# A fused attention and convolution kernel: the last attention slot computes its sums by transfers and most of its products in parts

## The chip, the cores and the metric

The kernel runs on one core of a Trainium2 chip. The metric is the device time of one execution in microseconds (us); less is better. The core has a matrix engine (PE, with its weight loads listed apart as PEld), a vector engine (DVE), an activation engine (ACT), a general engine (POOL) and a queue that issues transfers (SP). Each works through its own list in order; they meet at semaphores. Transfers run on 16 DMA engines and are issued by SP, ACT or POOL. PE writes into eight banks of PSUM, each 128 partitions by 512 columns in float32; everything else lives in SBUF or in main memory (HBM).

## The reference

The input x is (4, 64, 64, 256) in float32: four images of 4096 pixels (tokens) with 256 channels. Layer 0 is full attention inside an image, layer 1 a depthwise convolution with an MLP and a local attention. Cut to what matters:

```python
# layer 0, per image: N = 4096 tokens, q and k have 32 channels
q, k, v = x @ Wq + bq, x @ Wk + bk, x @ Wv + bv
attn = softmax(q @ k.T)                       # 4096 x 4096
x = gamma * (attn @ v) + x

# layer 1
perceived = depthwise_conv3x3(x, w_perc)      # 3 outputs for each of 256 channels
hid = gelu(perceived @ w_up1.T + b_up1)       # 768 -> 512
x_new = x + hid @ w_up2.T + b_up2             # 512 -> 256
qkv = x_new @ w_qkv.T + b_qkv
out = x_new + local_attention_3x3(qkv)
```

## The kernel before, in words

**Slots.** The tokens are cut into 32 blocks of 512 queries (eight image rows of one image). Slot s computes layer 0 for block s, and beside it layer 1 of earlier blocks: the convolution of block s - 2 on DVE, the MLP of block s - 3, the local attention of block s - 5. Lists of jobs, written out by hand, say which piece of layer 1 runs at which of the 16 points of a slot. There is no planner: the order of the Python program is the order on every engine. After slot 31 a tail runs the layer 1 that is left.

**A point of a slot.** The keys of the image come in eight blocks of 512, each worked in two half groups of 256 keys (two key tiles of 128). Half group n (0 to 15) is worked over several points. Two points ahead, PE computes the energies (line 418) and ACT the exponentials p (line 423). One point ahead, p is prepared: added to the sums, and split where that is wanted. At point n, PE multiplies p with the values (`product`, line 481), and the result of 16 half groups gathers in PSUM. At each point the order on PE is: energies of a later half group, the jobs of layer 1, the product. On DVE it is: what the jobs need, then `add_up` for the next half group, then some steps of the convolution (line 687).

**Products in one piece or in parts.** A product of float32 operands is recorded as two matmuls per 512 columns. In parts, p is split into a rounded high part (ACT, lines 428 and 437), a low part (DVE, lines 510 and 446) and a scaled gap (DVE, lines 520 and 447), and three matmuls of the float32r type replace the two; they need values that are split in the same way and read back from HBM. The high and low products go to two accumulators, the gaps to two more, so that a slot with parts holds four PSUM banks; `evacuate` (lines 564 and 567) joins them with two ACT and two DVE operations. `IN_PARTS` names the seven even half groups whose two tiles are both in parts (n = 2, 4, ..., 14); `ONE_IN_PARTS` names the odd ones of which the second tile is in parts, `BOTH_IN_PARTS` those of which the first tile is, too. `in_two_sums(s)`, `full(s)`, `in_parts` and `alone` decide which slots and half groups follow these lists. Before the change slot 31 follows none of them: all its products are in one piece.

**Sums of the weights.** The softmax needs the sum of p over all keys. In the middle slots the half groups that `by_dma` names are added by transfers that accumulate into two buffers (`send`, lines 498 and 500, issued by POOL); DVE adds only the last ones and the two buffers (lines 513, 516, 528, 529). Before the change slot 31 has none of these: DVE adds each of its 16 half groups (line 516 once, line 513 fourteen times).

**The values.** `project_v` computes the values of a block ahead of time, for the next image during the last slot of an image (for image 3 that is slot 23), and writes them to HBM: whole (`packed_v`, by ACT, lines 363 and 364), and in forms for the parts (`packed_h`, `packed_f`, `packed_o`, by POOL). For blocks 24 to 31 it writes the whole values of every pair of tiles, since slot 31 reads them all.

**Buffers.** Tiles have tags, and each tag a fixed ring of buffers: three for p, one each for ph, pl, pg, four for vs, two for xc, four for the convolution's outputs (perc). A tile that is asked for waits until the last reader of the buffer's previous tile is done. `late_tile` hands out thirds of one perc buffer, `spare` hands out other buffers that have gone out of use. PSUM: two banks for the energies, two banks m for jobs, four banks acc for the products. In the tail the energies' banks become two job banks more, and `turns` gives out the three kinds in rotation.

**Slot 31 and the tail.** Slot 31 has a longer list of jobs: it also runs the MLP of block 29 (`hidden_part`, line 800, at points 8 to 11; hid_a, hid_bc, hid_de and hid_gf are its products), so the convolution of block 29 has to be complete at point 8; then the convolution of block 30 (`upper`) runs, without its last row, which needs the result of slot 31. At the end the sums are closed (`partial_sums`, lines 547 and 550), one fold matmul (dps, line 576) and a reciprocal (line 579) give the factor, and `finish` (lines 590 and 596) scales the result. The tail then does the last row of block 30 and the convolution of block 31 on DVE, while PE runs what is ready of blocks 29 to 31.

Of the kernel before, what the change touches and what calls it, by code (L numbers as in the profile page):

```python
# [16 lines left out]
P = 128  # L17
# [5 lines left out]
NB = 512  # L23
RB = NB // W
WARM = 10
NBLK = N // NB
# [10 lines left out]
NHC = HID // P  # L37
# [5 lines left out]
NSLOT = B * NBLK  # L43
# [9 lines left out]
ONE_IN_PARTS = (1, 3, 5, 7, 9, 11, 13, 15)  # L53
# [5 lines left out]
LAG_PERC, LAG_HID, LAG_ATT = 2, 3, 5  # L59
# [3 lines left out]
def attention_then_perception_kernel(  # L63
# [37 lines left out]
    def unshifted():  # L101
# [6 lines left out]
        def tile_of(shape, tag, name, bufs=1):  # L108
            return pool.tile(shape, F32, tag=tag, name=name, bufs=bufs)

        def bank(tag, name):
            return psum.tile([P, NB], F32, tag=tag, name=name, bufs=dict(m=2, acc=2 * CH)[tag])
# [3 lines left out]
        turns = ["m"]  # L116
# [50 lines left out]
        for r in range(KR):  # L167
            m = near[r * KW : (r + 1) * KW]
# [48 lines left out]
        packed_o = tc.dram_tile([P, NSLOT, 2, 2, C], F32, name="packed_o")  # L217

        def in_two_sums(s):
            return 0 < s < NSLOT - 1 and s != LAG_PERC  # L220

        def full(s):
            return in_two_sums(s) and s > 1 and s % NBLK < NBLK - 1

        def in_parts(s, G, half):
            return in_two_sums(s) and 2 * G + half in IN_PARTS

        def alone(s, n):

            return [i for i, ns in enumerate((BOTH_IN_PARTS, ONE_IN_PARTS)) if full(s) and n in ns]  # L230

        def load_parts(to, s, which):
# [68 lines left out]
        def block(s, G):  # L301
            return s - s % NBLK + G
# [5 lines left out]
        def load_values(s, G):  # L308
            values[s, G] = tile_of([P, TPB, C], "v", f"v_{s}_{G}", 2)
            to = values[s, G].rearrange("p t c -> p (t c)")  # L310
            at = block(s, G)
            if not in_two_sums(s):
                nc.sync.dma_start(out=to, in_=packed_v[:, bass.ts(at, TPB * C)])
            elif full(s):
                nc.sync.dma_start(out=to, in_=packed_h[:, at])
            else:
                nc.sync.dma_start(out=to[:, : 2 * C], in_=packed_h[:, at, : 2 * C])
                nc.sync.dma_start(out=to[:, 2 * C :], in_=packed_v[:, bass.ts(2 * at + 1, 2 * C)])
# [23 lines left out]
        def project_v(s, pair, tag="m"):  # L342
            xc = staged[s]
            ps = bank(tag, f"v_{s}_{pair}")
            for i in range(2):
                for kin in range(CH):
                    nc.tensor.matmul(  # L347
                        ps[:, i * C : (i + 1) * C],
                        lhsT=xc[:, kin, bass.ts(2 * pair + i, P)], rhs=wv[:, kin, :],
                        start=(kin == 0), stop=(kin == CH - 1),  # L350
                    )
            of = ps.rearrange("p (t c) -> p t c", c=C)
            n = 2 * (s % NBLK) + pair
            split, one, both = (n in ns for ns in (IN_PARTS, ONE_IN_PARTS, BOTH_IN_PARTS))
            h = packed_h[:, s, bass.ts(pair, 2 * C)].rearrange("p (t c) -> p t c", c=C)
            if not split or s < NBLK or s >= NSLOT - NBLK:
                if s >= NBLK:
                    v = fresh(f"vs_{s}_{pair}")
                else:
                    if (0, s) not in values:  # L360
                        values[0, s] = tile_of([P, TPB, C], ("v", "vf")[s % 2], f"v_0_{s}", 2)
                    v = values[0, s][:, 2 * pair : 2 * pair + 2, :]
                nc.scalar.activation(v, of, AF.Identity, scale=SPLIT / (SPLIT + 1.0))  # L363
                nc.scalar.dma_start(
                    out=packed_v[:, bass.ts(2 * s + pair, 2 * C)],
                    in_=v.rearrange("p t c -> p (t c)"),
                )
                if not split and not both:
                    tiles = slice(0, 1 if one else 2)
                    nc.gpsimd.dma_start(out=h[:, tiles], in_=v[:, tiles])  # L370
            if not split and not one:
                return
            high = fresh(f"vh_{s}_{pair}")
            if split:
                lg = tile_of([P, 2, NB], "sent", f"vlg_{s}_{pair}")
                lg = lg.rearrange("p f (t c) -> p f t c", c=C)
                low, gap = lg[:, 0], lg[:, 1]
                to = h, packed_f[:, s].rearrange("p f (t c) -> p f t c", c=C)
            elif both:
                low, gap = (fresh(f"v{x}_{s}_{pair}") for x in "lg")  # L380
                lg = low
                to = h, packed_o[:, s, :, 0]
            else:
                high, of = high[:, 0:1], of[:, 1:2]
                lg = fresh(f"vlg_{s}_{pair}")
                low, gap = lg[:, 0:1], lg[:, 1:2]
                to = h[:, 1:2], packed_o[:, s, 1]
            nc.scalar.copy(low, of)
            nc.scalar.activation(high.bitcast(F32R), of, AF.Identity, scale=BELOW)
            nc.vector.tensor_tensor(low, low, high, ALU.subtract)  # L390
            nc.vector.scalar_tensor_tensor(gap, low, -SPLIT, high, ALU.mult, ALU.add)
            nc.vector.tensor_scalar(low, low, SPLIT, None, ALU.mult)
            for at, part in zip(to, (high, lg)):
                nc.gpsimd.dma_start(out=at, in_=part)
            if both:
                nc.gpsimd.dma_start(out=packed_o[:, s, :, 1], in_=gap)
# [88 lines left out]
                started[s].add(to)  # L485

        def by_dma(s, n):
            if full(s):
                return n in BY_DMA_IF_FULL and (n > 1 or s % NBLK > 0)
            return 0 < s < NSLOT - 1 and (s < 2 or s % NBLK < NBLK - 1) and n in BY_DMA  # L490

# [133 lines left out]
        percs, mixes, hids, hs = {}, {}, {}, {}  # L625
# [11 lines left out]
        def late_tile(name):  # L637

            if not thirds:
                t = perc_tile(name).rearrange("p s n -> p (s n)")  # L640
                thirds[:] = [t[:, i * NB : (i + 1) * NB] for i in range(3)]
            return thirds.pop(0)
# [4 lines left out]
                return tile_of([P, TPB, C], tag, name, 2).rearrange("p (a t) c -> p a (t c)", a=2)  # L647
            return tile_of([P, 2, NB], tag, name)

        spares = {NSLOT - 2: ["ph", "pl", "pg"], NSLOT - 1: ["v", "v", "vf"]}  # L650

        def perceive(s, steps):

            at = ring(s) - 1
            percs.setdefault(s, {})

            def begin(i):
                if s >= NSLOT - LAG_PERC:

                    if i % 2 == 0:  # L660
                        percs[s, i] = spare(s, f"perc_{s}_{i}")
                    percs[s][i] = percs[s, i - i % 2][:, i % 2, :]
                else:
                    upper, j = divmod(i, MULT)
                    if not upper:
                        mixes[s, j] = perc_tile(f"perc_{s}_{j}")
                    percs[s][i] = mixes[s, j][:, 2 * upper : 2 * upper + 2, :].rearrange(
                        "p s n -> p (s n)"
                    )
                tap_of(i, 0, 0, RB)  # L670

            def tap_of(i, tap, r0, r1):
                half, j = divmod(i, MULT)
                dy, dx = divmod(tap, 3)
                if s < NSLOT - LAG_PERC:
                    acc = percs[s][i][:, :RUN]
                    win = xp[:, half, bass.ds((at + dy) * WP + dx, RUN)]
                else:
                    acc = percs[s][i].rearrange("p (h w) -> p h w", w=W)[:, r0:r1, :]
                    win = xv[:, half, at + dy + r0 : at + dy + r1, dx : dx + W]  # L680
                wt = wperc[:, half, j, tap : tap + 1]
                if tap == 0:
                    nc.scalar.activation(  # L683
                        acc, win, AF.Identity, bias=bperc[:, half, j : j + 1], scale=wt
                    )
                else:
                    nc.vector.scalar_tensor_tensor(acc, win, wt, acc, ALU.mult, ALU.add)  # L687

            for i, tap, *rows in steps:
                if tap is None:  # L690
                    t = mixes[s, i][:, :, : ROWS - 2]
                    to, a, b, op = rows
                    nc.vector.tensor_tensor(t[:, to, :], t[:, a, :], t[:, b, :], op)  # L693
                    yield
                elif tap > 0:
                    tap_of(i, tap, *rows)
                    yield
                elif i not in percs[s]:
                    begin(i)
# [515 lines left out]
        for slot in range(NSLOT):  # L1215
# [52 lines left out]
            for point in range(points):  # L1268
                G, half = divmod(point, 2)
# [96 lines left out]
        def spread_bank(name):  # L1366
            return spread.tile([P, NB], F32, tag="s", name=name, bufs=2)

        turns[:] = [lambda name: bank("acc", name), spread_bank, "m"]
        last = NSLOT - 1  # L1370
        conv = perceive(last, whole)

# [454 lines left out]
```

## Time and profile before

| | |
|---|---|
| median of 3 runs | 3207.92 us (3205.68 to 3211.80) |
| profiled execution | 3206.14 us |
| its span, first to last instruction | 3204.3 us |
| busy over the span | PE 99%, DVE 91%, ACT 49%, POOL 24% |
| slot 30 (2862.0 to 2957.3) | PE busy 95.1 of 95.3 us, DVE 92.1, ACT 49.8 |
| slot 31 (2957.3 to 3091.0) | PE busy 133.7 of 133.7 us, DVE 112.8, ACT 46.5 |
| tail (3091.0 to 3204.3) | PE busy 103.4 of 113.3 us, DVE 69.1, ACT 30.5 |

How to read it: a line of the timeline gives the start, the length, the engine, the source line, the operation, output and inputs by the program's names, the number of instructions merged, and in brackets how long the engine was idle before and what ended that. The ends of matmuls are modelled and overlap with what follows, so the time that a group of matmuls takes is the distance from its start to the start of the next group. Times count from the start of the span. A mean over the span hides that slot 30, slot 31 and the tail are limited in different ways; the windows show them apart.

### The profile page before, as it was taken

The page shows a single profiled execution, that of the slowest core. Times are in us where ns is not written, and L with a number is a line of the kernel's source. Part 1 is how long each engine was busy: PE and PEld are TensorE (multiplying, and loading weights), DVE is VectorE, ACT ScalarE, POOL GpSimd, SP SyncE. Part 2 cuts the span into 40 slices and gives each one's busy share as a digit, 9 for nine tenths or more (in the row PEclk, how much of TensorE's full clock was granted, in tenths as well). Part 3 has the DMA queues.
Part 4 walks back from the last instruction along what each step waited for, and adds up shares of the span by engine and source line. Part 5 has one row for each costly group of instructions (what it writes and reads, how often), then busy time and mean ns, then how long its engine had stood idle before and what let it go on. Part 6 is the DMA issues. An engine that isn't in the chain of part 4 may idle for free.

```text
span 3204.3 us, 39564 instructions
## 1 busy us (share of the span) xinstructions
PE 3178.9 (99%) x12600; PEld 2269.4 (71%) x12600; DVE 2919.9 (91%) x4306; ACT 1580.8 (49%) x2173; POOL 753.5 (24%) x1052
## 2 busy tenths in 40 slices
PE   9999999999999999999999999999999999999998
PEld 5557777767777777776777777777677777777655
DVE  4878999998999999998999999999899999999894
ACT  4435555445555555544555555554555545555332
POOL 3301122222222221222122232211221223222121
PEclk9999999999999999999999999999999999999999
DMA  8768888877888888877888888886888888888100
GB/s 253 233 171 223 228 230 227 227 230 235 223 232 246 245 223 227 229 207 249 237 221 230 230 243 236 236 233 196 275 234 226 224 230 229 239 240 223 50 25 28
DMA packets 319446, 690.89 MB, mean 216 GB/s; under 512 B 100784, under 2 KB 101824, under 8 KB 319104
## 3 DMA queue, kind: packets, MB, share of 16 engines
q1 hardware_dynamic: 246608, 442.24, 43.0%
q0 software_dynamic: 64944, 232.59, 32.7%
q10 hardware_dynamic: 7680, 13.44, 1.2%
q8 instruction: 105, 1.72, 0.2%
q14 instruction: 109, 0.89, 0.1%
HBM read 419.01 MB, written 81.66 MB: 156 GB/s over the span
## 4 chain that ended last, share of the span: by engine, by line
PE 88%; DVE 8%; DMA 1%; issue 1%; ACT 1%; SPq 1%; ACTq 0%; DVEq 0%; POOL 0%; POOLq 0%
PE acc L481 43%; PE e L418 7%; PE dx L857 6%; PE hid_bc L800 5%; PE hid_gf L800 5%; PE hid_de L800 5%; PE lv L1022 3%; DVE perc L687 3%; PE g L953 3%; PE v L347 3%; PE lo L1155 3%; PE hid_a L800 2%; PE s L1062 2%; PE qk L272 1%; PE hid L832 1%
## 5 line engine op out<-in xcount | busy, mean ns | idle before, releaser
L687 DVE SCALAR_TENSOR_TENSOR perc<-xp,wb,perc 128x526 f32<-128x526 f32 (+1 forms) x1356 | 938.1, 759 | 0.4 <-ACT perc L683 0.2
L423 ACT ACTIVATE p<-e 128x1024 f32<-128x1024 f32 x512 | 524.3, 1024 | 487.6 <-PE e L418 387.9
L481 PE MATMUL acc<-p,v 128*128 128x512 f32 x1372 | 630.1, 594 | 0.2 <-ACT v L363 0.2
L500 POOL DMA_DIRECT2D sent<-p x304 | 257.9, 855 | 1347.3 <-ACT p L423 939.6
L481 PEld LDWEIGHTS acc<-p,v 128*128 128x128 f32 x1372 | 255.4, 190 | 242.6 <-issue 231.9
L418 PE MATMUL e<-qa,ka 128*128 128x512 f32 x1024 | 357.2, 430 | 4.5 <-DMA ka<-st 1.5
L428 ACT ACTIVATE ph<-p 128x1024 fp32r<-128x1024 f32 x203 | 215.1, 1059 | 197.8 <-PE acc L481 118.8
L510 DVE TENSOR_TENSOR pl<-p,ph 128x1024 fp32r<-128x1024 f32 x203 | 252.8, 1246 | 16.7 <-ACT ph L428 16.7
L481 PE MATMUL acc<-ph,v 128*128 128x512 f32 x812 | 264.5, 447 | 0.1
L520 DVE SCALAR_TENSOR_TENSOR pg<-pl,ph 128x1024 fp32r<-128x1024 f32 x203 | 253.8, 1250 | 11.6 <-PE e L418 0.5
L418 PEld LDWEIGHTS e<-qa,ka 128*128 128x128 f32 x1024 | 190.3, 188 | 86.6 <-issue 42.9
L857 PE MATMUL dx<-hid,wup 128*128 128x512 f32 x512 | 230.0, 592 | 0.0
L481 PE MATMUL acc<-pl,vf 128*128 128x512 f32 x812 | 223.2, 397 | 0.0
L481 PE MATMUL acc<-pg,vf 128*128 128x512 f32 x812 | 218.3, 391 | 3.0 <-DVE pg L520 3.0
L437 ACT ACTIVATE oh<-p 128x512 fp32r<-128x512 f32 x200 | 126.0, 630 | 140.6 <-DVE perc L687 61.3
L693 DVE TENSOR_TENSOR perc<-perc 128x262 f32<-128x262 f32 x360 | 179.6, 513 | 6.3
L481 PEld LDWEIGHTS acc<-ph,v 128*128 128x128 f32 x812 | 148.2, 189 | 51.5 <-issue 26.8
L481 PEld LDWEIGHTS acc<-pg,vf 128*128 128x128 f32 x812 | 152.3, 188 | 39.5 <-DVE pg L520 4.7
L481 PEld LDWEIGHTS acc<-pl,vf 128*128 128x128 f32 x812 | 152.9, 188 | 37.5
L823 ACT ACTIVATE hid<-hid,bup 128x512 f32<-128x512 f32 x120 | 80.2, 715 | 199.4 <-DVE hid L807 199.4
L481 PE MATMUL acc<-oh,v 128*128 128x512 f32 x400 | 174.6, 517 | 0.0
L857 PEld LDWEIGHTS dx<-hid,wup 128*128 128x128 f32 x512 | 96.8, 189 | 98.6 <-issue 93.5
(230 smaller groups left out, 5606.6 us busy)
## 6 DMA issues: line engine op xcount, KB each, us to landing
sent<-p POOLq DMA_DIRECT2D x356, 512.0 KB, 6.6
vf<-packed_f SPq DMA_DIRECT2D x203, 512.0 KB, 5.9
v<-packed_h SPq DMA_DIRECT2D x200, 512.0 KB, 4.8
vo<-packed_o SPq DMA_DIRECT2D x275, 256.0 KB, 4.5
ka<-packed SPq DMA_DIRECT2D x1016, 64.0 KB, 3.7
xp<-in_x SPq DMA_DIRECT2D x30, 528.0 KB, 7.3
packed_f<-vlg POOLq DMA_DIRECT2D x28, 512.0 KB, 4.4
xc<-in_x SPq DMA_DIRECT2D x56, 256.0 KB, 4.6
```

The costliest lines, as they stand in the source:

```text
L418: nc.tensor.matmul(e[:, i, :], lhsT=keys[s, G][:, bass.ts(2 * half + i, P)].bitcast(F32R), rhs=queries[s].bitcast(F32R), start=True, stop= ...
L423: nc.scalar.activation(p, e, AF.Exp)
L428: nc.scalar.activation(high.bitcast(F32R), weights[s, G, half], AF.Identity, scale=BELOW)
L437: nc.scalar.activation(high.bitcast(F32R), p, AF.Identity, scale=BELOW)
L481: nc.tensor.matmul(accs[s][to + c], lhsT=w[:, bass.ts(c, P)].bitcast(kind), rhs=x.bitcast(kind), start=to not in started[s], stop=last,)
L500: nc.gpsimd.dma_start(out=sent[s, even], in_=p, accum_op=ALU.add)
L510: nc.vector.tensor_tensor(low.bitcast(F32R), p, high, ALU.subtract)
L520: nc.vector.scalar_tensor_tensor(gap.bitcast(F32R), low, -SPLIT, high, ALU.mult, ALU.add)
L687: nc.vector.scalar_tensor_tensor(acc, win, wt, acc, ALU.mult, ALU.add)
L693: nc.vector.tensor_tensor(t[:, to, :], t[:, a, :], t[:, b, :], op)
L800: nc.tensor.matmul(ps[:, n * C : (n + 1) * C], lhsT=w(j), rhs=rows_of(mixes[s, j][:, kind, :]), start=(j == 0), stop=(j == MULT - 1),)
L857: nc.tensor.matmul(ps, lhsT=wup2[:, d, bass.ts(c, P)], rhs=hids[s][:, d, :], start=(d == 0), stop=(d == NHC - 1),)
```

## The change

Slot 31 now counts among the slots with two pairs of accumulators (`in_two_sums`). It follows from this and from the other edits that

- its seven even half groups n = 2, 4, ..., 14 are in parts, with their forms loaded from `packed_f`;
- the second tile of n = 1, 3, 5 and 7 is in parts (`last_one`), with its form loaded from `packed_o`; the second value tile of those comes with `packed_h`, and for n = 9, 11, 13, 15 the values are loaded in two transfers, from `packed_h` and `packed_v`;
- the sums of n = 0 to 13 go by 14 accumulating transfers, and DVE adds n = 14 and 15 and the two buffers;
- `evacuate` runs for slot 31, ahead of the reciprocal, and joins four accumulators;
- `project_v` no longer writes whole values for those pairs of blocks 25 to 31 whose tiles are both in parts: seven ACT operations and seven transfers of 256 KB fewer in slot 23;
- the six convolution outputs of block 30, which lay in the buffers ph, pl and pg, lie in three thirds of a perc buffer and three of the vs buffers;
- the rotation of banks in the tail begins with another kind.

In the order of the instructions PE has 76 rows more, DVE 32, SP 15 and POOL 14; the jobs of layer 1 keep their places.

```diff
         def in_two_sums(s):
-            return 0 < s < NSLOT - 1 and s != LAG_PERC
+            return 0 < s < NSLOT and s != LAG_PERC
 
+        def last_one(s, n):
+            return s == NSLOT - 1 and n < 2 * NHC
+
         def alone(s, n):
 
+            if last_one(s, n):
+                return [1] * (n in ONE_IN_PARTS)
             return [i for i, ns in enumerate((BOTH_IN_PARTS, ONE_IN_PARTS)) if full(s) and n in ns]
...
-            elif full(s):
+            elif full(s) or last_one(s, 2 * G + 1):
                 nc.sync.dma_start(out=to, in_=packed_h[:, at])
...
-            if not split or s < NBLK or s >= NSLOT - NBLK:
+            if not split or s < NBLK:
...
         def by_dma(s, n):
-            if full(s):
+            if full(s) or s == NSLOT - 1:
                 return n in BY_DMA_IF_FULL and (n > 1 or s % NBLK > 0)
...
-        spares = {NSLOT - 2: ["ph", "pl", "pg"], NSLOT - 1: ["v", "v", "vf"]}
+        spares = {NSLOT - 1: ["v", "v", "vf"]}
...
             def begin(i):
-                if s >= NSLOT - LAG_PERC:
+                if s == NSLOT - LAG_PERC:
+                    name = f"perc_{s}_{i}"
+                    percs[s][i] = late_tile(name) if i < 3 else tile_of([P, NB], "vs", name, 4)
+                elif s > NSLOT - LAG_PERC:
...
-        turns[:] = [lambda name: bank("acc", name), spread_bank, "m"]
+        turns[:] = [spread_bank, "m", lambda name: bank("acc", name)]
```

## The prediction

> **What bounds the kernel now.** First the page: the span, and which engine is full.
>
> ```profile
> span 3204.3 us, 39564 instructions
> PE 3178.9 (99%) x12600; PEld 2269.4 (71%) x12600; DVE 2919.9 (91%) x4306; ACT 1580.8 (49%) x2173; POOL 753.5 (24%) x1052
> ```
>
> PE is full and DVE is nearly so; a mean over the span does not say which of them ends the slot that is changed. Hence the busy times in three stretches: slot 30, slot 31 (the last attention slot), the tail.
>
> ```profile
> 2862.00:2957.30 95.30, 95.11 (x391) 70.72 (x390) 92.10 (x132) 49.80 (x67) 20.90 (x26) 1.00 0.86 233
> 2957.30:3091.00 133.70, 133.70 (x478) 86.02 (x477) 112.77 (x175) 46.52 (x66) 12.56 (x24) 1.00 0.15 48
> 3091.00:3204.30 113.30, 103.44 (x392) 62.87 (x391) 69.07 (x137) 30.47 (x54) 31.76 (x52) 0.97 0.05 20
> ```
>
> Columns: length; busy PE, PE's weight loads, DVE, ACT, POOL; clock; share of the DMA engines; GB/s. In slot 31 PE has no gap, DVE has 20.9 us free, and the DMA engines are at 0.15 where slot 30 has 0.86. Third, the timeline of PE: a plain half group in slot 31, then a half group in parts and one with a single key tile in parts in slot 30.
>
> ```profile
> 2997.93 3.60 PE L481 MATMUL acc<-p,v 128*128 128x512 f32 x8
> 3000.96 1.02 PE L418 MATMUL e<-qa,ka 128*128 128x512 f32 x2
> 3001.82 3.59 PE L857 MATMUL dx<-hid,wup 128*128 128x512 f32 x8
> ...
> 2908.76 3.60 PE L857 MATMUL dx<-hid,wup 128*128 128x512 f32 x8
> 2911.80 1.50 PE L481 MATMUL acc<-ph,v 128*128 128x512 f32 x4
> 2915.43 3.60 PE L857 MATMUL dx<-hid,wup 128*128 128x512 f32 x8
> 2918.87 1.88 PE L481 MATMUL acc<-p,v 128*128 128x512 f32 x4
> 2922.44 1.88 PE L953 MATMUL g<-h,wg 128*128 128x512 f32 x4
> ```
>
> The reader is to take starts, not durations. Fourth, DVE: what a split costs, and the place where it has most time to spare.
>
> ```profile
> 2896.32 1.22 DVE L510 TENSOR_TENSOR pl<-p,ph 128x1024 fp32r<-128x1024 f32 x1
> 2897.57 1.23 DVE L520 SCALAR_TENSOR_TENSOR pg<-pl,ph 128x1024 fp32r<-128x1024 f32 x1
> 2898.71 1.70 DVE L693 TENSOR_TENSOR perc<-perc 128x262 f32<-128x262 f32 x4
> ...
> 3026.54 0.75 DVE L687 SCALAR_TENSOR_TENSOR perc<-xp,wb,perc 128x512 f32<-128x512 f32 x1
> 3030.90 0.69 DVE L807 TENSOR_TENSOR hid<-hid_bc,hid 128x512 f32<-128x512 f32 x1 [3.62 <-PE hid_bc L800]
> ```
>
> Last, in slot 23 PE waits for ACT, at a bank that a value copy has yet to empty:
>
> ```profile
> 2305.30 1.46 PE L800 MATMUL hid_a<-perc,wup 128*128 128x256 f32 x6
> 2307.22 1.56 PE L800 MATMUL hid_bc<-perc,wup 128*128 128x256 f32 x6 [0.46 <-ACT vh L389]
> ```
>
> **The change, part by part.**
>
> *PE in slot 31.* A plain half group with the energies behind it takes 3001.82 - 2997.93 = 3.89 us; with the 3.43 us dx ahead of it (2994.50 to 2997.93), 7.32. In parts, dx to dx is 2915.43 - 2908.76 = 6.67: 0.65 less. With one tile in parts, 2922.44 - 2918.87 = 3.57: 0.32 less. Seven and four of them: 7 x 0.65 + 4 x 0.32 = 5.83 us off a queue that is never idle there.
>
> *DVE in slot 31.* A sum leaves the queue (1.13 us from start to start, 2976.28 to 2977.41) for each of n = 1 to 13; a split comes: 2898.71 - 2896.32 = 2.39 us for a half group, 1.33 for one tile (2901.91 to 2903.24). Up to the last mixing step of block 29's convolution (2967.9 to 3026.6, busy 52.90 of 58.70) that is 4 x (2.39 - 1.13) + 4 x (1.33 - 1.13) = 5.8 more: 58.7 us, so every wait of that stretch is used up and DVE ends at 3026.6 as before. PE comes to hid_a of block 29 at 3026.74 less 4 x 0.32 + 3 x 0.65, that is at 3023.5. Its third weight wants the LOWER output of perc_2, which is complete one tap (0.69) and four mixing steps (1.63) before 3026.6: 3024.3, against 3024.4 when PE gets to it. I count 0.3 us of stall. The bounds: none, and 3.2 us if the matmul waits for all four mixes. The program's order shows separate waits ahead of hid_a and of the two halves of hid_bc, so I stay near the lower.
>
> *The end of slot 31.* Behind point 8 the splits of n = 10, 12, 14 come, three sums go, and DVE adds two transferred sums and two evacuations: 3 x 1.26 - 3 x 1.13 + 2.48 + 1.29 = 4.2 us, within the 14 us it has free (50.45 busy of 64.50). But at the end it is in series. h of block 29 (L863) cannot start before dx is done: 3075.57 before, now 4 x 0.32 + 6 x 0.65 - 0.3 = 4.9 earlier, 3070.7. Behind it DVE does: h 0.79, split of n = 14 2.39, six taps 3.77, lo 1.35, lv 0.61, the closing sums as in slot 30 (2953.15 to 2957.65) 4.50, lv 0.61, transpose 0.73, reduce 0.69, the two L567 adds 1.29 (2960.12 to 2961.41): 16.7 us, so the reciprocal comes at 3087.4 instead of 3091.08. PE is through with n = 15 at 3090.68 - 5.53 = 3085.2 and waits, which costs nothing: the chain of waits goes through DVE from the reciprocal to 3128.07. Gain 3.65 of the 5.83.
>
> *The tail* keeps its work. Its chain on DVE (3091.08 to 3128) is one unbroken queue and moves whole. L590 reads o where it read the accumulator: 0.75 us per 512 columns (slot 30) against 0.68 per 448, the same. Four accumulators are now held instead of two, but until the L567 adds, ahead of the reciprocal, where L590 held two until 3097; the third job in the new order of banks wants one of them 3.7 us after dps. Bounds -0.5 to +1 us; I take 0.
>
> *ACT, POOL, SP, DMA in slot 31.* ACT gets 7 x 1.06 + 4 x 0.63 + 2 x 0.6 = 11.1 us beside 46.5 of 133.7. POOL gets 14 issues of 0.84, queued ahead of its local sum of block 27; block 27's total is needed 3 us after that ends. SP gets 15 more issues (seven forms, four single parts, four value blocks as two transfers), 6 us at 0.4, and ka waits behind them. All of this, three more single parts included, runs in slot 30 in points of 5.9 us with 0.19 us of PE idle; here points are 8. The closing sums wait for the landing of n = 12 and 13, 7.0 us after issue in slot 30 and here two points before. Cost nothing; without that cover, p's ring of three would hold exp, and then PE. The perception outputs of block 30 lie in buffers last read at points 3 and 7, and start at 7 or later: nothing.
>
> *Slot 23.* Seven ACT copies (0.60, and 0.4 before the next) and seven 256 KB transfers go. The nearest row is slot 15, the same slot without them: from one fold matmul (L576) to the next it takes 132.12 us, slot 7 131.91, slot 23 133.02. Bounds 0 and 1.1; I take 0.9, since PE is the bound from there on.
>
> *Sum.* 3.65 + 0.9 = 4.55. The profiled execution took 3206.14 (its span and 1.84 around it): 3201.6. It lies 1.8 under the median of the three runs, so as a median 3203.4, or 0.14% faster. I count 0.2% (6.4 us) as what a measurement can tell from no change; the three runs spread over 6.1.
>
> **The rivals.**
>
> *All of PE's saving arrives.* If the end of the slot is not in series on DVE and PE does not stall at point 8, 5.83 go, the evacuation gives back 0.9, slot 23 and shorter closing waits give 1 to 1.5: 3201.5 or less, faster by 0.2%. For it: the DVE chain beats PE only by 2 us. Against: dx and the closing sums are in one queue.
>
> *DVE becomes the bound.* If hid_a waits for all the mixes (3.2 us instead of 0.3), points 8 to 15 start later and DVE's closing queue with them: gain 0.7 in slot 31, 0.9 in slot 23, 3206.3. For it: the stretch has no wait left. Against: the separate waits.
>
> *POOL beside DVE.* A subtraction took 1.45 us at 2944.73 beside POOL's local sum, 0.69 at 2924.84 without. If issues of transfers act likewise, 14 x 0.84 us slow DVE by half: 3.5 us before point 8, 0.5 at the end, 3207.4. Against: pg at 2910.57 took 1.23 beside the issue at 2910.28. The Trainium skill (GPSIMD Engine Reference, Key points) says that GpSimd shares its SBUF interfaces with VectorE and contends with instructions that have two SBUF inputs. By that rule the splits suffer; the trace agrees for POOL's arithmetic and shows nothing for its issues.
>
> *Slower: convolution 29 late.* From point 8 on each further us of DVE goes to PE. If DVE's taps slow down while transfers fill the slot, it breaks even at 4.6 us and is slower by 0.2% from 11 us, 0.2 us on each of the 54 steps before hid_a: 3214.5 and more. For it: taps of up to 1.44 us exist. Against: their mean is 761 ns in slot 30 and 762 in slot 31, at DMA shares 0.86 and 0.15.
>
> **How the numbers follow.** Forecast 0.46, DVE bound 0.11, POOL 0.06: together 0.63 within 0.2%. All of the saving 0.21, faster. Late convolution 0.16, slower. The forecast's own range is 3201.5 to 3205.5; up to the other cases and with the runs' spread 3200.0 to 3210.0, which leaves out the slower case and little else.
>
> **What would show it.** Right: slot 31's starts 6.67 and 3.57 as in slot 30; PE idle under 0.5 us at hid_a of block 29; DVE without a wait from 2967 to there; dps idle some 1 us before the reduce; the reciprocal near 3086.5 (3087.4 less slot 23's 0.9); slot 23 at 132.1. Wrong: PE waits for pl, pg or perc in points 1 to 9; exp waiting for sent; SP late with ka; a tail longer than the 113.2 us from reciprocal to end.

## The result, and the profile after

The changed kernel takes 3202.10 us against 3206.82 us (medians of 22 executions each): a ratio of 0.9985 with a 95% interval from 0.9979 to 0.9992. That is 4.7 us less, with an interval from 2.6 to 6.7. The forecast, 4.55 us or 0.14% less, lies inside it, and the measured time lies inside the forecast's own range of 3201.5 to 3205.5. (The 3203.4 us of the forecast started from the median of three runs, 1.1 us above that of the 22.) The profiled execution has a span of 3200.8 us, against 3204.3.

The page, whose two lines answer to those of before (line numbers of the changed kernel are 5 to 8 higher):

```profile
span 3200.8 us, 39712 instructions
PE 3173.5 (99%) x12636; PEld 2276.7 (71%) x12636; DVE 2929.4 (92%) x4318; ACT 1587.7 (50%) x2179; POOL 766.2 (24%) x1066
```

PE is busy 5.4 us less and the span is 3.5 us shorter; DVE is busy 9.5 us more. The same three stretches (slot 30, slot 31, tail; the columns are length, then busy PE, weight loads, DVE, ACT, POOL, then clock, DMA share, GB/s):

```profile
2862.16:2957.46 95.30, 95.17 (x392) 70.80 (x391) 91.86 (x132) 49.54 (x67) 21.40 (x27) 1.00 0.86 231
2957.46:3088.90 131.44, 129.62 (x515) 92.44 (x514) 122.65 (x187) 57.02 (x79) 23.53 (x37) 1.00 0.54 142
3088.90:3200.80 111.90, 102.90 (x391) 62.58 (x389) 69.01 (x138) 30.47 (x54) 31.43 (x52) 0.98 0.05 20
```

Slot 31 is 2.3 us shorter. Its PE work fell from 133.70 to 129.62, by 4.1, and it now has gaps, 1.8 us of them. In the timeline of PE, half group n = 4 in parts, and then n = 5 with one tile in parts:

```profile
2994.47 3.60 PE L865 MATMUL dx<-hid,wup 128*128 128x512 f32 x8
2997.51 1.50 PE L486 MATMUL acc<-ph,v 128*128 128x512 f32 x4
...
3001.14 1.02 PE L865 MATMUL dx<-hid,wup 128*128 128x512 f32 x2
...
3006.12 1.91 PE L486 MATMUL acc<-p,v 128*128 128x512 f32 x4
...
3009.69 1.88 PE L961 MATMUL g<-h,wg 128*128 128x512 f32 x4
```

From dx to dx 6.67 us, and 3.57 us for the half group with one tile in parts: both as slot 30 had them. The matmuls gave what was forecast. PE lost part of it again at two places, which the timeline shows as waits (in brackets). Here lo is a product of the local attention, hid_a and hid_bc are products of the MLP of block 29, and perc is the convolution's output:

```profile
2989.26 1.77 PE L1163 MATMUL lo<-lp,lv 128*128 128x99 f32 x12 [0.66 <-DVE hid L815]
...
3024.72 1.82 PE L808 MATMUL hid_a<-perc,wup 128*128 128x256 f32 x6
3026.38 1.54 PE L808 MATMUL hid_bc<-perc,wup 128*128 128x256 f32 x6
...
3029.02 0.70 PE L808 MATMUL hid_bc<-perc,wmix 128*128 128x256 f32 x2 [0.25 <-DVE perc L701]
```

The first is a bank: lo of point 3 wants one that DVE empties with its second hid_de addition of block 28. The second is the convolution of block 29 at point 8; there a part of the wait lies inside the records (six matmuls of hid_a take 1.82 us, where the same six take 1.46 in slot 23 below), and so the busy time of PE fell by less than the matmuls gave. (Besides, PE has done 0.7 us of the tail's first product g before the reciprocal, where it had done 0.2.) DVE and POOL around it, and ahead of it the place where DVE waits in turn for lo; a tap (L695) is one step of the convolution, the mixing steps (L701) add its outputs for the MLP, and POOL's work is the masking (L1095) of the local attention's weights lp and their addition into `watched`:

```profile
2991.07 0.69 DVE L1176 SCALAR_TENSOR_TENSOR lo<-lo,lrden 128x512 f32<-128x512 f32 x1 [1.16 <-PE lo L1163]
...
3025.02 2.13 DVE L695 SCALAR_TENSOR_TENSOR perc<-xp,wb,perc 128x526 f32<-128x526 f32 x2
3025.50 1.09 POOL L1095 TENSOR_TENSOR lp<-lp,near 128x396 f32<-128x396 f32 x1 [6.75 <-ACT lp L1090]
...
3026.68 2.36 POOL L199 TENSOR_TENSOR watched<-watched,lp 128x128 f32<-128x128 f32 x4
3027.19 2.24 DVE L701 TENSOR_TENSOR perc<-perc 128x262 f32<-128x262 f32 x4
```

In the kernel before, DVE waited for lo, too, and POOL worked on these weights of block 28 after the mixing was over:

```profile
2990.77 0.69 DVE L1168 SCALAR_TENSOR_TENSOR lo<-lo,lrden 128x512 f32<-128x512 f32 x1 [0.85 <-PE lo L1155]
...
3023.44 1.44 DVE L687 SCALAR_TENSOR_TENSOR perc<-xp,wb,perc 128x526 f32<-128x526 f32 x2
3024.91 1.71 DVE L693 TENSOR_TENSOR perc<-perc 128x262 f32<-128x262 f32 x4
...
3027.52 0.95 POOL L1087 TENSOR_TENSOR lp<-lp,near 128x396 f32<-128x396 f32 x1 [62.77 <-ACT lp L1082]
3028.55 1.81 POOL L199 TENSOR_TENSOR watched<-watched,lp 128x128 f32<-128x128 f32 x4
```

The same four mixing steps take 2.24 instead of 1.71 us beside POOL, the two taps ahead of them 2.13 instead of 1.44, and POOL's own four additions 2.36 instead of 1.81. The two engines meet because the masking, which follows PE's scores by way of ACT, starts 2.0 us earlier than before (3025.50 against 3027.52), and DVE's taps 1.6 us later (3025.02 against 3023.44). That POOL is the cause shows in the rest of the trace after, too: of 23 such mixing steps that lie beside a masking for over nine tenths of their length, 22 take some 1.20 us, and none of the 310 others takes over 0.44. The end of the slot after the change:

```profile
3072.52 0.88 DVE L871 SCALAR_TENSOR_TENSOR h<-dx,bup,xp 128x256 f32<-128x256 f32 x2 [1.26 <-PE dx L865]
...
3087.95 0.37 PE L581 MATMUL dps<-parts,fold 128*128 128x16 f32 x2 [0.82 <-DVE parts L555]
...
3088.92 0.25 DVE L584 RECIPROCAL inverse<-dps 128x16 f32<-128x16 f32 x1
```

DVE waits for dx, then works 16.4 us without a gap to the reciprocal, and PE waits for it at the fold. Last, slot 23, where the wait of 0.46 us at hid_bc is gone:

```profile
2305.83 1.46 PE L808 MATMUL hid_a<-perc,wup 128*128 128x256 f32 x6
2307.13 1.46 PE L808 MATMUL hid_bc<-perc,wup 128*128 128x256 f32 x6
```

To set kernels side by side, five stages are read from each trace: **A**, slot 23, from one fold matmul (dps) to the next; **S24**, the slot behind it; **B**, from the fold matmul of slot 30 to the reciprocal of slot 31; **D**, from there to the end of the last DVE result; **E**, from there to the end of the span, which is the landing of the last output. The span is given to 0.1 us, so E is good to 0.05.

| kernel | A | S24 | B | D | E |
|---|---|---|---|---|---|
| before | 133.02 | 94.79 | 128.20 | 106.79 | 6.43 |
| after | 131.92 | 94.42 | 125.88 | 106.79 | 5.09 |
| after, again | 131.93 | 94.46 | 125.94 | 106.77 | 5.27 |
| after, third (E9) | 132.98 | 94.44 | 125.92 | 106.79 | 5.30 |
| E1 sums alone | 133.08 | 94.79 | 128.19 | 106.80 | 5.17 |
| E2 parts without sums | 131.91 | 94.46 | 136.78 | 106.78 | 6.50 |
| E3 whole values again | 133.44 | 94.78 | 125.90 | 106.78 | 5.18 |
| E4 buffers alone | 132.97 | 94.78 | 128.20 | 106.77 | 6.32 |
| E5 n = 7 in one piece | 131.91 | 94.44 | 125.27 | 106.77 | 5.12 |
| E6 single parts at 1, 5, 9 | 132.06 | 94.44 | 124.45 | 106.80 | 5.26 |
| E7 n = 14 in one piece | 132.99 | 94.41 | 125.45 | 106.76 | 5.31 |
| E8 without POOL's watch | 131.92 | 94.39 | 125.39 | 106.75 | 5.17 |

B, S24 and D repeat to 0.1 us. E takes 5.1 to 6.5 us, and not by the kernel (E1, which is the kernel before but for its sums, has 5.17, and E2, which has the changed tail, 6.50), so the 1.3 us between the first pair of traces is scatter. The stages that repeat add up to 2.3 (B) + 1.1 (A) + 0.36 (S24) = 3.8 us, inside the measured interval. The trace after also holds a late transfer in slot 26 (a wait of 1.04 us for ka at 2570.95) that no second trace of the same kernel has; it is not counted.

### The profile page after: what moved, and what is told of

It is laid out like the page before. It is cut to its first block, busy times and chain, and to the rows that moved or that the text cites. A ratio compares the mean times of both kernels' runs of the same rounds, so it can differ in the third digit from the quotient of the medians.

```text
span 3200.8 us, 39712 instructions
## 1 busy us (share of the span) xinstructions
PE 3173.5 (99%) x12636; PEld 2276.7 (71%) x12636; DVE 2929.4 (92%) x4318; ACT 1587.7 (50%) x2179; POOL 766.2 (24%) x1066
## 4 chain that ended last, share of the span: by engine, by line
PE 84%; DVE 10%; DMA 2%; issue 1%; SPq 1%; ACT 1%; ACTq 0%; DVEq 0%; POOL 0%; POOLq 0%
PE acc L486 41%; PE e L423 6%; PE dx L865 6%; PE hid_bc L808 5%; PE hid_gf L808 5%; PE hid_de L808 5%; DVE perc L695 4%; PE v L352 3%; PE lv L1030 3%; PE lo L1163 3%; PE g L961 3%; PE hid_a L808 2%; PE s L1070 2%; DMA ka<-packed 2%; PE qk L277 1%
## 5 line engine op out<-in xcount | busy, mean ns | idle before, releaser
L695 DVE SCALAR_TENSOR_TENSOR perc<-xp,wb,perc 128x526 f32<-128x526 f32 (+1 forms) x1356 | 937.6, 756 | 0.6 <-ACT perc L691 0.2
L505 POOL DMA_DIRECT2D sent<-p x316 | 268.1, 855 | 1396.2 <-ACT p L428 954.4
L486 PE MATMUL acc<-p,v 128*128 128x512 f32 x1300 | 598.0, 595 | 0.2 <-ACT v L368 0.2
L486 PEld LDWEIGHTS acc<-p,v 128*128 128x128 f32 x1300 | 241.9, 190 | 227.6 <-issue 217.3
L433 ACT ACTIVATE ph<-p 128x1024 fp32r<-128x1024 f32 x210 | 222.5, 1060 | 207.4 <-PE acc L486 124.8
L515 DVE TENSOR_TENSOR pl<-p,ph 128x1024 fp32r<-128x1024 f32 x210 | 261.5, 1245 | 16.7 <-ACT ph L433 16.7
L486 PE MATMUL acc<-ph,v 128*128 128x512 f32 x840 | 273.7, 447 | 0.2
L525 DVE SCALAR_TENSOR_TENSOR pg<-pl,ph 128x1024 fp32r<-128x1024 f32 x210 | 262.4, 1249 | 11.8 <-PE c L1011 0.5
L486 PE MATMUL acc<-pl,vf 128*128 128x512 f32 x840 | 231.0, 397 | 0.0
L486 PE MATMUL acc<-pg,vf 128*128 128x512 f32 x840 | 225.9, 391 | 3.3 <-DVE pg L525 3.3
L701 DVE TENSOR_TENSOR perc<-perc 128x262 f32<-128x262 f32 x360 | 179.9, 514 | 6.3
```

The costliest lines, as they stand in the source:

```text
L433: nc.scalar.activation(high.bitcast(F32R), weights[s, G, half], AF.Identity, scale=BELOW)
L486: nc.tensor.matmul(accs[s][to + c], lhsT=w[:, bass.ts(c, P)].bitcast(kind), rhs=x.bitcast(kind), start=to not in started[s], stop=last,)
L505: nc.gpsimd.dma_start(out=sent[s, even], in_=p, accum_op=ALU.add)
L515: nc.vector.tensor_tensor(low.bitcast(F32R), p, high, ALU.subtract)
L525: nc.vector.scalar_tensor_tensor(gap.bitcast(F32R), low, -SPLIT, high, ALU.mult, ALU.add)
```

## The experiments

The theory at the start: PE's saving in slot 31 is 5.8 us as forecast, the end of the slot waits for DVE's closing queue, and PE loses some 2 us more than forecast to waits for DVE at lo and at hid_a; slot 23 gains by the copies that are gone. The rivals: the gain comes from the sums that leave DVE; from the buffers and the rotation; or the loss lies in the closing queue alone.

**The changed kernel again (E0).** No edit.

> The changed kernel once more, unaltered, for the spread of the stage times. Stages: A is slot 23 between its two fold matmuls (dps), 133.02 us before and 131.92 after; B is from the fold matmul of slot 30 to the reciprocal of slot 31, 128.20 before and 125.88 after; D is from that reciprocal to the last DVE result, 106.79 in both; E is from there to the end of the span, 6.43 before and 5.09 after. My theory (stages A and B carry the gain): A 131.9, B 125.9, D 106.8, each within 0.2; E free, anything from 5 to 6.5, since only the landing of the last output is in it. Rival (the new order of banks shortens the tail): E again 5.1.

Measured 3201.29 us beside 3205.28 for the kernel before, one execution each, and B, S24, A and D within 0.06 of the first trace. These differences are then properties of the kernel.

**E1, the sums alone.** The kernel before, with slot 31's sums by transfers and nothing else:

```diff
         def by_dma(s, n):
-            if full(s):
+            if full(s) or s == NSLOT - 1:
```

> The kernel before with one part of the change: 14 sums of slot 31 by transfers, no product in parts. My theory (PE's queue bounds slot 31): DVE loses 13 additions of 1.13 us and gains two of 1.24, and nothing comes of it, because PE is never idle there: B 128.2, within 0.3. Rival (DVE's additions are what the slot pays for): B falls by 2 us or more, at most by the 12 us that leave DVE.

Measured 3204.84 beside 3205.28, and B 128.19, as before the change. The page of E1:

```profile
PE 3177.4 (99%) x12600; PEld 2269.4 (71%) x12600; DVE 2906.1 (91%) x4294; ACT 1580.6 (49%) x2173; POOL 766.1 (24%) x1066
```

DVE's busy time is 13.8 us below that of before (2919.9), and the slot is not shorter by 0.1 us. PE set its pace, and 14 issues by POOL and 14 transfers cost it nothing. The slot's time does not test the rival that issues slow DVE, since DVE had time to spare; DVE's rows do. In E1's trace 54 taps of 526 columns lie beside an issue for over nine tenths of their length, and their median is 0.76 us, that of the 748 beside no work of POOL. For the mixing steps it is 0.43 us in both cases. That rival falls.

**E2, the parts without the sums.** The changed kernel, with slot 31's sums on DVE:

```diff
         def by_dma(s, n):
-            if full(s) or s == NSLOT - 1:
+            if full(s):
```

> The changed kernel with the sums of slot 31 on DVE, as before the change; the products stay in parts. My theory (in points 0 to 7 DVE has no time left, so each us more there is a stall of PE at hid_a of block 29): eight additions of 1.13 us make B 9 us longer, 134 to 136, with PE waiting for DVE at hid_a or in the points ahead of it. Rival (DVE's waits of before had room for both, PE's saving comes anyway): B 125.5 to 127.

Measured 3212.47 beside 3205.28, and B 136.78, 8.6 us above the kernel before and a little above what was expected. Three of PE's waits in the timeline of E2:

```profile
2990.25 2.71 PE L1163 MATMUL lo<-lp,lv 128*128 128x99 f32 x12 [2.81 <-DVE hid L815]
...
3033.79 0.70 PE L808 MATMUL hid_a<-perc,wup 128*128 128x256 f32 x2 [3.65 <-DVE perc L695]
...
3091.34 1.99 PE L1030 MATMUL lv<-wlv,h 128*128 128x256 f32 x8 [2.00 <-DVE lo L1176]
```

All of PE's waits in the slot add up to 10.6 us, and every one of these three ends with DVE. With the splits on top of the sums DVE is what PE mostly waits for in slot 31, and the parts without the sums by transfer make the kernel slower. The sums by transfers are worth nothing alone and 10.9 us under the parts (136.78 - 125.9).

**E3, the whole values of blocks 24 to 31 written again.**

```diff
-            if not split or s < NBLK:
+            if not split or s < NBLK or s >= NSLOT - NBLK:
```

> The changed kernel, writing the whole values of blocks 25 to 31 in slot 23 again (seven ACT copies and seven 256 KB transfers, which nobody reads). My theory: A back at 133.0 (from 131.9), with PE waiting for vh ahead of hid_bc; B stays at 125.9. Rival (the 1.1 us of stage A are scatter between executions): A stays at 131.9 to 132.2.

Measured 3204.14 beside 3205.28; A 133.44 (0.4 above what was expected) and S24 94.78, B 125.90. The wait is back:

```profile
2308.79 1.56 PE L808 MATMUL hid_bc<-perc,wup 128*128 128x256 f32 x6 [0.70 <-ACT vh L394]
```

The gains of slots 23 and 24 both come from the copies and transfers that are gone. The 0.36 us of slot 24 lie at one product: PE waits there for a low part that DVE splits (`acc<-vo`, at 2381.28 in the trace before, where that matmul starts 0.83 us behind the one ahead of it; after the change it is 0.61, and the rest comes with the next matmuls).

**E4, the buffers and the rotation alone**, on the kernel before:

```diff
-        spares = {NSLOT - 2: ["ph", "pl", "pg"], NSLOT - 1: ["v", "v", "vf"]}
+        spares = {NSLOT - 1: ["v", "v", "vf"]}
...
-        turns[:] = [lambda name: bank("acc", name), spread_bank, "m"]
+        turns[:] = [spread_bank, "m", lambda name: bank("acc", name)]
```

and the branch of `begin` as in the change.

> The kernel before with only the perception outputs of block 30 in the perc and vs buffers and the new order of banks in the tail. My theory (these carry no time): A 133.0 to 133.4, B 128.2, D 106.8, each within 0.2. Rival (the places or the order of banks give something of their own): B or D moves by 0.5 us or more.

Measured 3203.45 beside 3205.48 in one execution each; the stages A, S24, B and D are those of before to 0.05 us, so the 2 us are scatter outside them. The buffers only make room for the tiles ph, pl and pg of slot 31.

**E5, half group n = 7 in one piece**, the last single tile ahead of hid_a:

```diff
         def last_one(s, n):
-            return s == NSLOT - 1 and n < 2 * NHC
+            return s == NSLOT - 1 and n < 2 * NHC - 1
```

> The changed kernel with the second key tile of n = 7 in one piece again. PE then works 0.32 us more, DVE 1.33 us less in the point ahead of hid_a of block 29. My theory (in the changed kernel PE waits 0.95 us there because DVE is late): the wait goes, B falls by about 0.6 to 125.3. Rival (each tile in parts is worth its PE time): B rises by 0.3 to 126.2.

Measured 3199.13 beside 3205.48; B 125.27, with 125.3 expected. The wait at hid_a is gone from the trace. PE has 0.32 us more to do, and the slot is 0.63 us shorter: this tile in parts cost more in DVE's 1.33 us than it saved.

**E7, half group n = 14 in one piece**, so that its split leaves DVE's closing queue. It needs the whole values of that pair of block 31, one copy more in slot 23:

```diff
         def in_parts(s, G, half):
-            return in_two_sums(s) and 2 * G + half in IN_PARTS
+            return in_two_sums(s) and 2 * G + half in IN_PARTS and (s, G, half) != (NSLOT - 1, NG - 1, 0)
...
-            if not split or s < NBLK:
+            if not split or s < NBLK or s == NSLOT - 1:
```

The load of these values and the last product in parts follow.

> The changed kernel with the half group n = 14 in one piece again (and the whole values of block 31 written for it in slot 23). PE then works 0.65 us more, DVE's closing queue is 2.39 us shorter. My theory (at the end of slot 31 PE and DVE are level within 1 us, and the two L572 adds follow whichever is later): the wait of the fold matmul goes (0.82 us), B stays within 0.2 of 125.9. Rivals: each half group in parts is worth its PE time, B 126.5; DVE's closing queue is the bound by more than 1 us, B 123.5 to 125.2.

Measured 3200.11 beside 3205.48; B 125.45. The expectation, 125.9 within 0.2, was wrong, and the figure lies above the 125.2 of the rival, too: the reciprocal came 0.43 us earlier and the fold no longer waited. Against 2.39 us less on DVE, PE has 0.65 more and becomes the one that ends the slot, since DVE's last additions (L572) now wait for its product; the split of n = 14 is a small loss where it stands. And A is back at 132.99, with the wait at the same matmul as before. Both waits, in order of time:

```profile
2305.58 1.56 PE L808 MATMUL hid_bc<-perc,wup 128*128 128x256 f32 x6 [0.47 <-ACT vh L394]
...
3084.87 0.69 DVE L572 TENSOR_TENSOR o<-acc,o 128x512 f32<-128x512 f32 x1 [0.60 <-PE acc L486]
```

One of the seven copies, the last, right ahead of hid_bc, is thus worth all of slot 23's 1.1 us, as far as one trace shows it. S24 stays at 94.41, so the 0.36 us there hang on other copies than this one.

**E8, without POOL's watch of block 28.** POOL's additions of the local attention's weights into `watched` are left out for this block; the masking of the weights (L1095) stays:

```diff
-            if DIRECT <= s < NSLOT - 2:
+            if DIRECT < s < NSLOT - 2:
```

> The changed kernel without POOL's watch over the local weights of block 28 (two times four additions into the watched tile, part of the guard against overflow, are left out). In the changed kernel DVE's four mixing steps of perc_2 of block 29 took 2.24 us beside the first of these, and 1.71 before, without. My theory (POOL's arithmetic slows DVE's two-input operations): the four steps take 1.7 to 1.8, PE's wait at hid_bc of block 29 is 0.4 to 0.5 shorter, B 125.4 to 125.5. Rival (the transfers of the slot slow them): 2.2 and 125.9 as before.

Measured 3201.85 beside 3205.48; B 125.39. In the timeline of E8, DVE's taps beside the masking, an issue of a transfer by POOL, and the mixing beside no arithmetic:

```profile
3024.78 2.14 DVE L695 SCALAR_TENSOR_TENSOR perc<-xp,wb,perc 128x526 f32<-128x526 f32 x2
3025.25 1.10 POOL L1095 TENSOR_TENSOR lp<-lp,near 128x396 f32<-128x396 f32 x1 [6.75 <-ACT lp L1090]
3026.31 0.85 POOL L505 DMA_DIRECT2D sent<-p  x1
3026.95 1.71 DVE L701 TENSOR_TENSOR perc<-perc 128x262 f32<-128x262 f32 x4
```

The mixing is back at 1.71 us, and B is 0.5 us shorter. The taps, still beside the masking, are still at 2.14. POOL's additions, which the change moved to where DVE is late, thus made up about half of the 0.95 us lost at hid_a. What the masking adds to that was not tested by leaving it out.

**E9 and E6, other single tiles.** The last two were timed on one chip, with 11 executions each. E9 is the changed kernel; E6 puts n = 1, 5 and 9 in parts in place of 1, 3, 5 and 7:

```diff
         def last_one(s, n):
-            return s == NSLOT - 1 and n < 2 * NHC
+            return s == NSLOT - 1 and n in (1, 5, 9)
```

and loads the values of n = 9 in three transfers, since only their second tile is used in parts.

> The changed kernel, unaltered, so that the next kernel can be set beside it on one chip. Both theories expect what it showed before: 125.9 us from the folding matmul of slot 30 to the reciprocal of slot 31, 131.9 us in slot 23, 94.4 us in slot 24, and a time some 4 us under the kernel before.

> Of block 31's single key tiles n = 1, 5 and 9 are in parts, in place of n = 1, 3, 5 and 7: the energies of n = 3 and n = 7 come before hid_a and before the projection's lo again as float32 work, and n = 9 saves its 0.32 us later, where no wait stands. Theory, the waits of PE eat what those two tiles save: the waits at lo and at hid_a go or fall under 0.3 us together, and from the folding matmul of slot 30 to the reciprocal of slot 31 it takes 124.4 to 124.9 us, at least 1 us under the changed kernel beside it, with 131.9 us in slot 23 still. Rival, PE's time goes by the number of key tiles in parts alone: one tile fewer in parts costs 0.32 us, 126.2 us. Rival, the closing queue of DVE sets the reciprocal: n = 9 in parts brings its hidden sums and sums later on DVE, and the end stays at 125.3 or later, as where n = 7 alone was left out, with PE ahead of it at the folding matmul.

E9 took 3201.60 us (median; ratio 0.9985 with an interval from 0.9976 to 0.9994), E6 3199.31 (0.9976, from 0.9967 to 0.9985), beside 3206.11 for the kernel before (21 executions). The two intervals overlap, but the stage agrees: B is 124.45 in E6 against 125.92, with 124.4 to 124.9 expected; the rival by which each key tile counts for its PE time would have given 126.2, and the one by which the closing queue alone sets the end 125.3 or later. The timeline of E6 at the places that waited:

```profile
2988.32 1.70 PE L1170 MATMUL lo<-lp,lv 128*128 128x99 f32 x12
...
3024.39 1.46 PE L815 MATMUL hid_a<-perc,wup 128*128 128x256 f32 x6
3025.69 1.46 PE L815 MATMUL hid_bc<-perc,wup 128*128 128x256 f32 x6
3026.98 1.46 PE L815 MATMUL hid_bc<-perc,wmix 128*128 128x256 f32 x6
...
3070.92 0.88 DVE L878 SCALAR_TENSOR_TENSOR h<-dx,bup,xp 128x256 f32<-128x256 f32 x2 [1.25 <-PE dx L872]
...
3086.38 0.37 PE L588 MATMUL dps<-parts,fold 128*128 128x16 f32 x2 [0.83 <-DVE parts L562]
...
3087.34 0.25 DVE L591 RECIPROCAL inverse<-dps 128x16 f32<-128x16 f32 x1
```

No wait stands at lo or at hid_a any more; h comes 1.4 us earlier within the slot, and the same 16.4 us later the reciprocal. So two statements hold at once: DVE's closing queue ends the slot, and what starts that queue is PE with its waits. E6 gains 6.8 us on the kernel before (5.1 of them in the stages A, S24 and B), and is the fastest of the kernels that were timed over many executions.

E9's trace has A at 132.98. Its wait there is another than that of before: PE waits 0.81 us for ACT, and ACT for a transfer, as ACT's timeline shows:

```profile
2310.14 0.63 ACT L442 ACTIVATE oh<-p 128x512 fp32r<-128x512 f32 x1 [1.20 <-DMA packed_h<-vh]
```

A buffer of the value forms is waited for until its transfer has landed. Of the seven traces without the seven copies, six have A at 131.9 to 132.1 and this one 1.06 more: slot 23 is not shorter in every execution.

## Why the prediction was right, and where not

**PE's saving in slot 31: right.** 6.67 and 3.57 us from start to start, the forecast figures.

**The stall of PE: the term that was mis-sized.** "I count 0.3 us of stall" was 1.8 us of waits, and 2.0 with all that is missing. This is read from h of block 29, which follows PE's dx. In the kernel before it lies 112.69 us behind the fold of slot 30 (3075.57 - 2962.88), after the change 109.48 (3072.52 - 2963.04): 3.21 us earlier, where the six half groups and four single tiles that lie ahead of it give 5.18 (6 x 0.65 + 4 x 0.32). In E6, with no wait there, it is 108.03, 4.66 earlier, where six and three give 4.86. Set against E6, the two places of the changed kernel cost 0.89 us at lo (from the start of the last hid_gf group to the product behind lo, 3.72 against 2.83) and 0.95 at hid_a and hid_bc (from hid_a to the product, 4.65 against 3.70). The rest, 0.1 to 0.2, is missing in E6, too, and is no wait.

Two things were missing from that step. The first is the bank at lo: the prediction followed only the convolution's data to hid_a, and so missed that lo must wait until DVE has emptied a bank. DVE then waits for lo in its turn, 1.16 us, in the very stretch that had no time left. "DVE without a wait from 2967 to there" was wrong by that one wait (and two of 0.1). Only 0.3 of the 1.16 follow from PE's wait at the bank: DVE waited 0.85 for lo in the kernel before, and 0.84 in E6, where lo waits for nothing. What was missed is mostly that DVE must wait for this product at all, however full its queue is. The second is POOL's arithmetic, which now falls beside the last taps and the mixing: 0.69 + 0.53 = 1.22 us. The 1.16 and the 1.22 together are 2.4 of the 2.7 us by which the mixing ends later than forecast (3029.4, less the 0.16 by which the trace runs later, against 3026.6). The step "DVE ends at 3026.6 as before" took the durations of before for granted, in a stretch in which the order of POOL against DVE had changed. One of the prediction's own signs of being wrong came, therefore: PE waits for perc at point 8.

**The end of the slot: right.** DVE's closing queue ends the slot, with PE waiting at the fold; it took 16.4 us (3072.52 to 3088.92) against 16.7 forecast. The forecast gain of 3.65, less 1.7 of further loss, plus 0.3 for the shorter queue, is 2.3, as measured. E7 adds that the queue ends the slot by little: with 2.39 us taken off it, the end came only 0.43 earlier, and PE was the later of the two. E6, without the stall and with one tile fewer, gains 3.75 (128.20 - 124.45).

**The tail, ACT, SP and DMA: right.** D is the same to 0.05 us in all traces, and E1 and E4 show that neither the transfers of the sums nor the buffers cost the slot or the tail anything by themselves.

**Slot 23: right in size, and incomplete.** 0.9 forecast, 1.1 found in most traces, on one copy of the seven as far as E7 shows. Slot 24 gives 0.36 more, which the prediction did not look for: 94.79 with the copies, 94.4 without, in all twelve traces. Which copy does that was not settled.

**The sum.** 3.65 + 0.9 = 4.55 was forecast, and 2.3 + 1.1 + 0.36 = 3.8 is found. One term was too high by 1.35 and two too low by 0.56 together, so part of the error cancelled. That the median difference of 4.7 comes so close to 4.55 is luck, and no confirmation of the terms.

**The rivals.** That all of PE's saving arrives was wrong on both its conditions. That DVE becomes the bound (a gain of 0.7 in the slot) was nearer than its chance said: the slot lost 2.0 us where this rival charged 3.2, though only 0.95 of them at hid_a, the rival's own place. That POOL slows DVE was right of its arithmetic and wrong of what it was put to, the issues, beside which the taps of E1 keep their 0.76 us. The row that the prediction read for it is another: the subtraction of 1.45 us at 2944.73 lay beside the masking (2944.42 to 2945.64), not beside the local sum, and the one of 0.69 us at 2924.84 lay beside an issue (2924.40 to 2925.25). The rule of the Trainium skill (GPSIMD Engine Reference, Key points) that GpSimd contends with VectorE instructions that have two SBUF inputs agrees with these rows: taps and mixing both have two, and E8 gets 0.53 us back by leaving out the additions beside the mixing. A late convolution that makes the kernel slower did not come; E2 shows what it looks like, with the sums left on DVE.

## What to carry to other kernels

Where two engines are both nearly full, follow every wait between them in both directions, those for banks as well as those for data: time that is free in a queue cannot all be filled with work if part of it is a wait for the other engine's product. Moving work off an engine that is not the bound is worth nothing alone (E1) and can still be what makes the next change pay (E2). A split that saves one engine 0.32 us and costs the other 1.33 belongs where the second one has time: one such tile fewer, and the others at other places, gained 1.4 us more.

## What was not expected of the hardware

POOL's arithmetic and DVE's slow each other where they overlap: of the two taps of 526 columns the one beside the masking took 1.46 us and the one ahead of it 0.76; four mixing steps of 262 columns went from 1.71 to 2.24, POOL's four additions of 128 columns from 1.81 to 2.36. Issues of transfers by POOL, some 0.85 us each, showed no such effect on the operations of DVE beside them (0.76 us for 54 taps in E1), and two taps of 512 columns beside a memset by POOL took 0.74 us in the trace after, against 0.75 for those beside nothing.
